# A projection's products and its weight's load moved behind the support's, in the first row group of a two-layer graph-attention kernel

## The chip, the cores and the metric

The kernel runs on one core of one Trainium2 chip. The metric is the device time of one execution in microseconds (us). A profiled execution gives a trace beside it, from which the views below are taken. The engines are PE (TensorE; PEld is its weight load), DVE (VectorE), ACT (ScalarE), POOL (GpSimd) and SP (SyncE, which here only issues DMAs). L841 means line 841 of the kernel before.

## The reference, cut to what matters

Two graph-attention layers over 4096 nodes with 512 features, each followed by a residual and a layer norm. Only the first layer's projections are touched by the change:

```python
support = (x @ weight).reshape(N, H, D)          # 4096x512 by 512x512, 4 heads of 128
f1, f2  = support . weight_u,  support . weight_v  # two numbers per node and head
attn    = masked softmax of leaky_relu(f1 + f2), masked by adj
out     = attn @ support + bias + x @ proj_w + proj_b
x1      = layernorm(x + out)
...                                              # then layer 2: masked multi-head attention, layernorm
```

So `x` is multiplied by two 512x512 weights. The product with `weight` (called "s", the support) feeds everything that follows in layer 1. The product with `proj_w` (called "b", the base) is only added at the end of layer 1; the kernel adds an identity to `proj_w` first, so that the base is the residual too.

## The kernel before, in words

**Stages.** Stage 1 computes supports, bases and attention factors, in eight groups of 512 rows (`g` from 0 to 7, loop at L902). Stage 2 is layer 1's attention: 16 passes (4 windows of 1024 rows, 4 heads) whose products are L1062. Then come layer 2's projections (L1171, L1178) and its attention (L1113, L1375). Beside stage 1 the adjacency is read, cast to 16 bits by a DMA that POOL issues (`narrow`, L589) and transposed by a DMA that SP issues (`turn_in0`, L595), for stage 2.

**A group of stage 1.** Each 512x512x512 product is made from seven half-size products instead of eight (Strassen's scheme). They have the numbers 1 to 7; `("s", 5)` is number 5 of the support. One of them is four matmuls in the source, which the trace shows as eight instructions of 128x256. The products take, besides plain blocks of `x` and of the weights, sums of blocks:

- `combine_x(g, 0..3)` makes four sums of blocks of the group's transposed `x`: 0 and 1 on DVE (L792, L794), 2 and 3 on POOL (L796, L799). Products 5, 6, 7 and 3 need the sums 0, 1, 2 and 3.
- `combine_w` makes four sums of weight blocks once, in the order 5, 6, 7, 4 (L758): for the support on DVE, for the base on POOL. Products 5, 6, 7 and 4 need one each. `add_identity` (L885) must have been over `proj_w` before the base's sums are made; it is 16 additions of 32x32 on POOL.
- Product 2 is added to product 1 in the same PSUM tile, 3 to 5, and 4 to 7. Between the two, the first must have been copied out or read: 1 and 5 by ACT (L858), 7 by DVE (L864). Then ACT (2, L860) and DVE (6, L862; 3 and 4, L869) take the results into the support tile `s4` or the base tile `base`; the last block also needs an addition on POOL (L866). There are six PSUM tiles for the eight that a group uses.
- `dots` (L812) computes the two attention numbers of each node and head from `s4`, on DVE, in four calls of eight operations; each call needs one block of `s4`, the third one the block that POOL's L866 finishes. `turn_x` (L735) transposes the next group's `x` on DVE, in four steps; product 1 of that group needs the first two, its `combine_x` all four.
- POOL adds the bias `bb` to `base` (L873), and SP stores it (L875).

The order on every engine is written out by hand: the lists `begin` (group 0), `usual` and `end` give the order of the 14 products of a group, with counter `k`; each product brings its own copies and additions, and the other steps hang on `k`. An engine takes its instructions in that order. `Later` holds functions until a number of its steps has passed; `step()` is called at four values of `k`.

**Loads at the start.** SP issues the first group's `x` in two halves of four DMAs, and then the `x` of groups 1 and 2. ACT issues sixteen DMAs for the two weights (first half of `weight`, first half of `proj_w`, second halves in the same order; a half is four DMAs of 128 KB) and three more for `uv` and `bias`, all ahead of its first computing instruction. DMAs that SP and ACT issue share eight completion counters, so that a later DMA waits on its engine until an earlier one has landed.

Of the kernel before, what the change touches and what calls it, by code (L numbers as in the profile page):

```python
# [8 lines left out]
F32 = mybir.dt.float32  # L9
# [9 lines left out]
P = 128  # L19
# [410 lines left out]
def tile_gat_then_masked_attention(  # L430
# [16 lines left out]
    nc = tc.nc  # L447
    N, D = x.shape
# [4 lines left out]
    NG = N // G  # L453
# [35 lines left out]
    base_d = [dram.tile([P, GT, D], F32, name=f"base_d{g}") for g in range(NG)]  # L489
# [59 lines left out]
    later = Later()  # L549
# [20 lines left out]
    with tc.tile_pool(name="l0", bufs=NG) as l0, \  # L570
# [71 lines left out]
        with tc.tile_pool(name="l0s", bufs=2) as sp:  # L642
            w_sb, pw_sb = (sp.tile([P, KC, D], F32, name=n, bufs=1) for n in ("w_sb", "pw_sb"))
# [3 lines left out]
            def load_x(g, b0=0, b1=G // SQ):  # L647

                if g not in ys:
                    ys[g] = sp.tile([P, G // SQ, P], F32, name="y_sb", bufs=3)  # L650
                for a in range(NQ):
                    nc.sync.dma_start(
                        ys[g][a * SQ:(a + 1) * SQ, b0:b1, :],
                        x[g * G + b0 * SQ:g * G + b1 * SQ, a * P:(a + 1) * P].rearrange(
                            "(b r) f -> r b f", r=SQ))

            def load_w0(dst, src, c):

                for a in range(NQ):
                    f = a * P + 2 * c * SQ  # L660
                    nc.scalar.dma_start(
                        dst[a * SQ:(a + 1) * SQ, 2 * c:2 * c + 2, :],
                        src[f:f + 2 * SQ, :].rearrange("(k r) d -> r k d", r=SQ))

            bb = sp.tile([P, D], F32, name="bb", bufs=1)
            for n in range(2):
                load_x(0, n * HG // SQ, (n + 1) * HG // SQ)
            for c in range(2):
                for dst, src in ((w_sb, weight), (pw_sb, proj_w)):
                    load_w0(dst, src, c)  # L670
            for k, src in enumerate((weight_u, weight_v)):
                nc.scalar.dma_start(uv[:, k, :], on_all_partitions(src, D))
            nc.scalar.dma_start(bb, on_all_partitions(bias, D))
# [127 lines left out]
            def x_of(g, i):  # L801
                if i in (1, 2, 4):
                    return x_block(g, *{1: (0, 0), 2: (0, 1), 4: (1, 1)}[i])
                return x_s[g][{5: 0, 6: 1, 7: 2, 3: 3}[i]]
# [11 lines left out]
            tiles, base = {}, {}  # L816
# [13 lines left out]
            def product(g, s4, kind, i):  # L830

                if i in (1, 5, 6, 7):
                    tiles[kind, i] = op.tile([P, G], F32, name="o_ps")
                out = tiles[kind, {2: 1, 3: 5, 4: 7}.get(i, i)]
                more = i in (2, 3, 4)
                xb, wb = x_of(g, i), w_of(kind, i)
                for t in range(2):
                    for c in range(2):  # L840
                        nc.tensor.matmul(out[:, t * HD:(t + 1) * HD], xb[:, c, t * P:(t + 1) * P],  # L841
                                         wb[:, c, :], start=not more and t == 0 and c == 0,
                                         stop=c == 1, skip_group_check=True)
                if i == 1:
                    if kind == "b":
                        for n in range(2):
                            base[n] = sp.tile([P, 2, D], F32, name="base", bufs=2)
                    elif g == NG - 1:
                        places = room("y_sb").rearrange("p s c r -> p s (c r)")
                        sb.update({("s", 1): places[:, 0], ("s", 5): places[:, 1],  # L850
                                   ("b", 1): places[:, 2], ("b", 5): places[:, 3]})
                    else:
                        sb.update({("s", 1): room("z"), ("s", 5): room("z"),
                                   ("b", 1): room("az"), ("b", 5): room("az")})
                u2, p5 = sb[kind, 1], sb[kind, 5]
                last = block_of(kind, s4, 1, 1)
                if i in (1, 5):
                    nc.scalar.activation(sb[kind, i], out, AF.Copy)  # L858
                elif i == 2:
                    nc.scalar.activation(block_of(kind, s4, 0, 0), as_block(out, kind), AF.Copy)  # L860
                elif i == 6:
                    nc.vector.tensor_tensor(u2, out, u2, op=ALU.add)  # L862
                elif i == 7:
                    nc.vector.tensor_tensor(last, as_block(out, kind), as_block(u2, kind),  # L864
                                            op=ALU.add)
                    nc.gpsimd.tensor_tensor(last, last, as_block(p5, kind), op=ALU.add)  # L866
                else:
                    n, m = (0, 1) if i == 3 else (1, 0)
                    nc.vector.tensor_tensor(block_of(kind, s4, n, m), as_block(out, kind),  # L869
                                            as_block(u2, kind), op=ALU.add)  # L870
                if kind == "b" and i in (3, 4):
                    n = (3, 4).index(i)
                    nc.gpsimd.tensor_tensor(base[n], base[n],  # L873
                                            bb[:, None, :].to_broadcast([P, 2, D]), op=ALU.add)
                    nc.sync.dma_start(base_d[g][:, 2 * n:2 * n + 2, :], base[n])  # L875

            for n in range(2):
                for c in range(KC):
# [1 line left out]
            def add_identity(m):  # L880
                for c in range(KC):
                    for a in range(2 * m, 2 * m + 2):
                        q, f = slice(a * SQ, (a + 1) * SQ), a * P + c * SQ
                        d = pw_sb[q, c, f:f + SQ]
                        nc.gpsimd.tensor_tensor(d, d, ident[q, q], op=ALU.add)  # L885

            add_identity(0)
            combine_x(0, 0)
            combine_w(nc.vector, "s", (5,))
            for i in (1, 2, 3):  # L890
                combine_x(0, i)
            combine_w(nc.vector, "s", (6, 7, 4))
            add_identity(1)
            combine_w(nc.gpsimd, "b", (5, 6, 7, 4))
            nc.gpsimd.dma_start(bb, on_all_partitions(proj_b, D), accum_op=ALU.add)
            uv_ps = [xp.tile([P, H0, D0], F32, name="x_ps") for _ in range(2)]
            usual = [(kind, i) for i in (1, 5, 2, 6, 7, 3, 4) for kind in ("s", "b")]
            begin = [("s", 1), ("b", 1), ("s", 2), ("b", 2), ("s", 5), ("s", 6), ("s", 7),
                     ("b", 5), ("s", 3), ("b", 6), ("s", 4), ("b", 7), ("b", 3), ("b", 4)]
            end = [("s", 1), ("b", 1), ("s", 5), ("s", 2), ("s", 6), ("s", 7), ("b", 5),  # L900
                   ("s", 3), ("b", 2), ("s", 4), ("b", 6), ("b", 7), ("b", 3), ("b", 4)]
            for g in range(NG):  # L902
                fs[g] = l0.tile([P, 2, GT, H0], F32, name="f")
                s4 = sp.tile([P, H0, GT, W0], F32, name="s4")
                plan = end if g == NG - 1 else usual if g else begin
                todo = {}
                for i, wait, n, m in ((2, 1, 0, 0), (3, 0, 0, 1), (7, 3, 1, 1), (4, 0, 1, 0)):
                    todo.setdefault(plan.index(("s", i)) + wait, []).append((n, m))
                for k, (kind, i) in enumerate(plan):
                    if k in (0, 3, 7, 10):  # L910
                        t = (0, 3, 7, 10).index(k)
                        if t == 1 and g + 2 < NG:
                            load_x(g + 2)
                        for fn in beside.get(g * GT + t, []):
                            fn()
                    product(g, s4, kind, i)
                    if g == 0 and k == 2:
                        for n in range(2):
                            nc.scalar.activation(uv_ps[n], uv[:, n, :].rearrange(
                                "p (h d) -> p h d", h=H0), AF.Copy)  # L920
                    for nm in todo.get(k, ()):
                        dots(g, s4, *nm)
                    first = 0 if g else 10
                    if g + 1 < NG and first <= k < first + KC:
                        turn_x(g + 1, k - first)
                    if g + 1 < NG and (6 <= k < 10 if g else k == 13):
                        for n in (k - 6,) if g else range(4):
                            combine_x(g + 1, n)
                    if k in (2, 6, 9, 13):
                        later.step()  # L930
                xTs.pop(g)
                x_s.pop(g)
                if g + 1 < NG:
                    later.at(1, lambda g=g, s4=s4: factors(g, s4))
                else:
                    factors(g, s4)
# [18 lines left out]
        with wait_by_tile("l0v", 2) as vp:  # L955
# [95 lines left out]
            for n, (w, h, j) in enumerate(steps):  # L1051
# [8 lines left out]
                s = sup[w * H0 + h, j // GT][:, j % GT, :]  # L1060
# [11 lines left out]
    with wait_by_tile("l1", 1) as l1, wait_by_tile("l1a", 2) as lp, \  # L1072
# [46 lines left out]
        with wait_by_tile("l1s", 2) as sp:  # L1119
# [125 lines left out]
            for pair in range(NG // 2):  # L1245
# [4 lines left out]
                if pair == 0:  # L1250
                    combine_features(nc.vector, 0, 3)
                    combine_features(nc.vector, 0, 4)
                    for i in (5, 1, 6, 7):
                        todo = beside.setdefault(order[order.index(i) - 3], [])
# [36 lines left out]
        with wait_by_tile("l1w", 2) as wp, wait_by_tile("l1o", 1, space=PSUM) as op:  # L1291
            NB = 3
            later = Later()
# [274 lines left out]
```

## Time and profile before

| | |
|---|---|
| three runs | 3372.57 us median (3371.79 to 3374.13) |
| the profiled execution | 3370.89 us, of which the span that its trace covers is 3369.1 us |
| PE busy | 3324.9 us, 99% of the span |
| DVE, POOL, ACT busy | 70%, 66%, 59% |
| granted TensorE clock, mean | 0.996 of full speed |
| group 0 of stage 1 | first matmul at 8.76 us, group 1's first at 48.28 us |
| stage 2's first products | 226.99 us; without further stalls from 263.45 us |

Every time below is counted from the span's start. In the timeline a row is: start, duration, engine, line, operation, tile written and tiles read, count; in brackets the idle time of the engine ahead of it, and what ended that idle time. A "q" after an engine marks instructions of its queue, such as the issue of a DMA. In the list of waits a row is: who waited, for whom, then total us, number of times, longest. In the table by windows a row is: window, its length, then for PE, PEld, DVE, ACT and POOL the busy us with the number of instructions, then the granted PE clock, the share of the 16 DMA engines that was busy and the GB/s moved.

### The profile page before, as it was taken

What the parts mean: (1) busy time and instruction counts of PE and PEld (TensorE: products, weight loads), DVE (VectorE), ACT (ScalarE), POOL (GpSimd) and SP (SyncE); (2) the same over time, 40 slices, a digit from 0 to 9 for tenths busy, and PEclk for the clock granted to TensorE, in tenths of its full rate; (3) what the DMA queues carried; (4) which work ended last, traced back from release to release, by engine and by line L of the source; (5) the groups of instructions that cost most, each with busy time, mean ns of one, the idle gap of its engine ahead of it and who ended that gap; (6) DMA issues with size and microseconds to landing.
All of it is one profiled execution on the core that took longest, in us unless ns stands there. A gap on an engine that the chain in (4) does not pass through costs nothing.

```text
span 3369.1 us, 66595 instructions
## 1 busy us (share of the span) xinstructions
PE 3324.9 (99%) x27050; PEld 1950.0 (58%) x27050; DVE 2358.5 (70%) x2892; ACT 1987.4 (59%) x2463; POOL 2226.1 (66%) x1590
## 2 busy tenths in 40 slices
PE   7999999999999999999999999999999999999998
PEld 6889999999999855543333333333333333333332
DVE  5678899898899711157766667676676767667676
ACT  1247877878776421156665656666566656656554
POOL 5540031040030275579999999999999999999996
PEclk9999999999999999999999999999999999999999
DMA  7969869769451443388989898889989889898884
GB/s 162 228 153 177 202 188 218 150 155 215 138 140 64 92 171 112 115 224 195 210 192 222 226 211 195 204 200 237 216 188 213 194 203 253 189 210 190 209 196 111
DMA packets 399054, 620.41 MB, mean 184 GB/s; under 512 B 166672, under 2 KB 247568, under 8 KB 397712
## 3 DMA queue, kind: packets, MB, share of 16 engines
q0 software_dynamic: 97520, 258.77, 42.3%
q1 hardware_dynamic: 298976, 353.35, 34.5%
q10 hardware_dynamic: 2240, 3.93, 0.5%
q8 instruction: 215, 3.52, 0.4%
q14 instruction: 103, 0.84, 0.1%
HBM read 315.87 MB, written 117.64 MB: 129 GB/s over the span
## 4 chain that ended last, share of the span: by engine, by line
PE 89%; DMA 1%; DVE 1%; POOL 1%; issue 0%; ACT 0%; POOLq 0%; DVEq 0%; ACTq 0%
PE o_ps L1062 26%; PE o_ps L1375 25%; PE s_ps L1113 25%; PE s_ps L1178 5%; PE s_ps L1439 3%; PE s_ps L1171 3%; DMA p<-p 1%; PE s_ps L1394 1%; PE x_ps L1043 0%; POOL q_sum L1350 0%; DVE p L637 0%; DMA stage<-adj_d 0%; DVE p L1507 0%; PE x_ps L1171 0%; POOL p L1360 0%
## 5 line engine op out<-in xcount | busy, mean ns | idle before, releaser
L1350 POOL TENSOR_TENSOR q_sum<-q_sum,p 128x1024 f32<-128x1024 f32 x538 | 1376.2, 2558 | 62.6 <-DMA p<-p 38.9
L1330 DVE TENSOR_TENSOR p<-s_ps,adjT 128x1024 f32<-128x1024 f32 x896 | 1043.5, 1215 | 467.2 <-ACT s_ps L1327 443.6
L1327 ACT ACTIVATE s_ps<-s_ps 128x1024 f32<-128x1024 f32 x1021 | 967.2, 1006 | 594.9 <-PE s_ps L1113 594.2
L1375 PE MATMUL o_ps<-p,v_sb 64*64 64x512 f32 x8192 | 943.6, 590 | 0.0
L1113 PE MATMUL s_ps<-q_sb,k_sb 64*64 64x512 f32 x8192 | 943.1, 589 | 0.5 <-DVE p L1330 0.4
L1062 PE MATMUL o_ps<-sup_t,p 128*128 128x129 f32 x8192 | 920.9, 275 | 2.4 <-DVE p L637 2.2
L1062 PEld LDWEIGHTS o_ps<-sup_t,p 128*128 128x128 f32 x8192 | 918.5, 192 | 3.1 <-DVE p L637 3.0
L637 DVE SCALAR_TENSOR_TENSOR p<-fr_t,dj,az 128x1024 f32<-128x1024 f32 x512 | 655.7, 1291 | 78.8 <-PE o_ps L1062 50.6
L1113 PEld LDWEIGHTS s_ps<-q_sb,k_sb 64*64 64x64 f32 x8192 | 312.5, 133 | 567.0 <-issue 453.1
L1375 PEld LDWEIGHTS o_ps<-p,v_sb 64*64 64x64 f32 x8192 | 310.3, 133 | 570.6 <-issue 560.6
L628 ACT ACTIVATE z<-fr_t,f 128x1024 fp8e4<-128x1024 f32 x512 | 558.1, 1144 | 125.9 <-DVE az L632 125.4
L1360 POOL DMA_DIRECT2D p<-p x412 | 438.5, 1304 | 10.2 <-PE o_ps L1375 8.5
L1026 POOL DMA_DIRECT2D agg<-base_d x32 | 28.7, 1206 | 516.0 <-ACT agg L1012 515.8
L1330 DVE TENSOR_TENSOR p<-s_ps,md 128x1024 f32<-128x1024 f32 x128 | 150.7, 1216 | 67.3 <-ACT s_ps L1327 62.7
L632 DVE TENSOR_TENSOR az<-adjT,z 128x512 int32<-128x512 int32 x256 | 175.6, 686 | 11.2 <-ACT z L628 10.4
L588 POOL COPY seen<-token 128x1 f32<-128x1 f32 x24 | 13.4, 557 | 246.2 <-DVE token L586 246.2
L1185 ACT ACTIVATE sb<-s_ps 128x1024 f32<-128x1024 f32 x35 | 35.8, 1024 | 191.8 <-PE s_ps L1178 129.1
L601 ACT ACTIVATE adjT<-stage 128x1024 fp8e4<-128x1024 bf16 x128 | 130.4, 1049 | 6.3 <-DMA stage<-adj_d 6.3
L1200 POOL TENSOR_TENSOR sb<-sb,sb 128x1024 f32<-128x1024 f32 x36 | 84.9, 2374 | 71.8 <-ACT sb L1185 71.8
L1224 DVE COPY k_sb<-s_ps 128x1024 f32<-128x1024 f32 x12 | 14.7, 1225 | 140.7 <-PE s_ps L1178 90.6
L1439 PE MATMUL s_ps<-wo_sb,on 128*128 128x512 f32 x240 | 110.8, 604 | 0.0
L1409 ACT ACTIVATE r<-r_h 32x256 f32<-32x256 f32 x248 | 102.3, 412 | 2.9
(176 smaller groups left out, 2135.4 us busy)
## 6 DMA issues: line engine op xcount, KB each, us to landing
p<-p POOLq DMA_DIRECT2D x412, 512.0 KB, 9.1
k_sb<-k_d SPq DMA_DIRECT2D x128, 512.0 KB
v_sb<-v_d SPq DMA_DIRECT2D x128, 512.0 KB
adj_d<-in_adj_dram POOLq DMA_DIRECT2D x32, 1024.0 KB, 11.3
sup_t<-sup_d SPq DMA_DIRECT2D x120, 258.0 KB
fr_t<-fr_d SPq DMA_DIRECT2D x16, 1024.0 KB
adjT_d<-adjT SPq DMA_DIRECT2D x32, 512.0 KB
adjT<-adjT_d SPq DMA_DIRECT2D x32, 512.0 KB
```

What stands on the lines that cost most here:

```text
L628: nc.scalar.activation(z[:, k, :], fr[:, 0, :], AF.Sign, bias=fs[j // GT][:, 0, (j + k) % GT, h:h + 1], saturate=False)
L632: nc.vector.tensor_tensor(az.bitcast(I32), adjT[w, j // CJ][:, j % CJ:j % CJ + 2, :].bitcast(I32), z.bitcast(I32), op=ALU.bitwise_and)
L637: nc.vector.scalar_tensor_tensor(p, fr[:, 1, :], dj[j // GT][:, j % GT, h:h + 1], az_t[w, h, j // 2][:, j % 2, :], op0=ALU.max, op1=ALU.mult)
L1062: nc.tensor.matmul(o[t // BK][:, t % BK, :], p[:, t * P:(t + 1) * P], s, start=(j == 0 and t % BK == 0), stop=(j == NT - 1), skip_group_ch ...
L1113: nc.tensor.matmul(s[c:c + MS, e, :], k[r, a + c:a + c + MS], qt[g, m][r, :], start=True, stop=True)
L1178: nc.tensor.matmul(half, a[:, c, n * P:(n + 1) * P], x[:, c, :], start=not more and c == 0, stop=c == 1, skip_group_check=True)
L1327: nc.scalar.activation(s, s, AF.Exp)
L1330: nc.vector.tensor_tensor(p, s, keep[:, None, :].to_broadcast([P, HP, G]), op=ALU.mult)
L1350: nc.gpsimd.tensor_tensor(q, q, p, op=ALU.add)
L1360: later.at(2, lambda: nc.gpsimd.dma_start(a, b, accum_op=ALU.add))
L1375: nc.tensor.matmul(o[c, n, :], v[r, j % CH, c], p[r, e, :], start=(j == 0), stop=(j == NT - 1))
L1439: nc.tensor.matmul(s, on_t[g][:, m, t * P:(t + 1) * P], wo_sb[:, m, :], start=(m == 0), stop=(m == NP1 - 1))
```

## The change

- `begin` lists all seven support products first, then the seven of the base, each in the order 1, 2, 5, 6, 7, 3, 4. Before, the two kinds alternated. The copy of `uv` to PSUM moves from `k` = 2 to `k` = 6, and the four calls of `dots` of group 0 to `k` = 7, 8, 9 and 10.
- `proj_w` is loaded from SP's queue, after `x` of group 0 and ahead of `x` of groups 1 and 2. ACT's queue keeps `weight`, `uv` and `bias`.
- All 16 additions of the identity come after POOL's `combine_x(0, 2)` and `(0, 3)`; eight of them stood ahead of those before.
- The store of a `base` half is handed to `Later` with one step, and the last of the four steps of a group is called at `k` = 12 instead of 13 (with one more after group 7). `base` has three buffers instead of two.

```diff
-            for c in range(2):
-                for dst, src in ((w_sb, weight), (pw_sb, proj_w)):
-                    load_w0(dst, src, c)
+            for queue, dst, src in ((nc.scalar, w_sb, weight), (nc.sync, pw_sb, proj_w)):
+                for c in range(2):
+                    load_w0(queue, dst, src, c)
...
-                            base[n] = sp.tile([P, 2, D], F32, name="base", bufs=2)
+                            base[n] = sp.tile([P, 2, D], F32, name="base", bufs=3)
...
-                    nc.sync.dma_start(base_d[g][:, 2 * n:2 * n + 2, :], base[n])
+                    later.at(1, lambda t=base[n]: nc.sync.dma_start(
+                        base_d[g][:, 2 * n:2 * n + 2, :], t))
...
-            add_identity(0)
             combine_x(0, 0)
             combine_w(nc.vector, "s", (5,))
             for i in (1, 2, 3):
                 combine_x(0, i)
             combine_w(nc.vector, "s", (6, 7, 4))
-            add_identity(1)
+            for m in range(2):
+                add_identity(m)
             combine_w(nc.gpsimd, "b", (5, 6, 7, 4))
...
-            begin = [("s", 1), ("b", 1), ("s", 2), ("b", 2), ("s", 5), ("s", 6), ("s", 7),
-                     ("b", 5), ("s", 3), ("b", 6), ("s", 4), ("b", 7), ("b", 3), ("b", 4)]
+            begin = [(kind, i) for kind in ("s", "b") for i in (1, 2, 5, 6, 7, 3, 4)]
...
-                for i, wait, n, m in ((2, 1, 0, 0), (3, 0, 0, 1), (7, 3, 1, 1), (4, 0, 1, 0)):
-                    todo.setdefault(plan.index(("s", i)) + wait, []).append((n, m))
+                for k, (i, wait, n, m) in enumerate(
+                        ((2, 1, 0, 0), (3, 0, 0, 1), (7, 3, 1, 1), (4, 0, 1, 0))):
+                    todo.setdefault(plan.index(("s", i)) + wait if g else 7 + k, []).append((n, m))
...
-                    if g == 0 and k == 2:
+                    if g == 0 and k == 6:
                         for n in range(2):
                             nc.scalar.activation(uv_ps[n], uv[:, n, :].rearrange(
                                 "p (h d) -> p h d", h=H0), AF.Copy)
...
-                    if k in (2, 6, 9, 13):
+                    if k in (2, 6, 9, 12):
                         later.step()
                 xTs.pop(g)
                 x_s.pop(g)
+                if g + 1 == NG:
+                    later.step()
```

More of the change, by code (lines that the diff above doesn't have):

```diff
@@ L655, in load_x, with load_w0 @@
                             "(b r) f -> r b f", r=SQ))
-            def load_w0(dst, src, c):
+            def load_w0(queue, dst, src, c):
                 for a in range(NQ):
                     f = a * P + 2 * c * SQ
-                    nc.scalar.dma_start(
+                    queue.dma_start(
                         dst[a * SQ:(a + 1) * SQ, 2 * c:2 * c + 2, :],
```

## The prediction

> **What bounds the kernel now.** I read the page's busy shares first, then the table by windows cut at the stages, then the waits and the timeline of the first 60 us, and the chain of waits up to 270 us. The page says that PE is the bound; the table says where it isn't:
>
> ```profile
> PE 3324.9 (99%) x27050; PEld 1950.0 (58%) x27050; DVE 2358.5 (70%) x2892; ACT 1987.4 (59%) x2463; POOL 2226.1 (66%) x1590
> ```
> ```profile
> 0.00:48.28 48.28, 30.13 (x112) 24.64 (x113) 19.93 (x88) 5.77 (x9) 16.91 (x35) 0.89 0.84 153
> 48.28:215.90 167.62, 167.62 (x777) 147.25 (x775) 110.19 (x517) 51.16 (x94) 100.28 (x89) 1.00 0.91 202
> 215.90:263.45 47.55, 37.68 (x298) 36.36 (x297) 38.86 (x82) 27.37 (x31) 14.83 (x10) 0.89 0.66 158
> 263.45:1157.00 893.55, 893.43 (x8000) 893.23 (x8000) 805.90 (x907) 680.25 (x761) 122.41 (x169) 1.00 0.69 154
> ```
>
> Group 0 ends at 48.28. Up to there PE is busy 30.13 of 48.28 us; from there to 215.9 it never stops, so groups 1 to 7 follow group 0's end one for one. What the change reorders lies in that first window, and what holds PE there is in the timeline:
>
> ```profile
> 8.76 3.78 PE L841 MATMUL o_ps<-w_sb,xT 128*128 128x256 f32 x8 [8.76 <-DVE xT L735]
> 12.79 2.79 PE L841 MATMUL o_ps<-pw_sb,xT 128*128 128x256 f32 x8 [0.26 <-DMA pw_sb<-in_L_gnn_proj_w_dram]
> 21.10 1.28 ACT L858 ACT_TABLE_LOAD   x1 [21.10 <-DMA pw_sb<-in_L_gnn_proj_w_dram]
> 22.40 0.60 ACT L858 ACTIVATE z<-o_ps 128x512 f32<-128x512 f32 x1
> 23.05 3.78 PE L841 MATMUL o_ps<-w_sb,xT 128*128 128x256 f32 x8 [7.46 <-ACT z L858]
> ...
> 46.48 1.97 PE L841 MATMUL o_ps<-more_w,xT 128*128 128x256 f32 x8 [1.68 <-DVE base L864]
> ```
>
> PE does s1 and b1, then stands 7.46 us, because s2 goes into s1's PSUM tile and ACT has not copied s1 out; ACT can't before 21.10, because it is still issuing loads. From 23.05 PE runs nearly without a stop to 48.28 (1.68 us for DVE at b4), the first 5 us of it at half the clock.
>
> **What the Trainium skill says.** (1) "TensorE: Matmul & The Clock Gate", Part 1: the PE clock is at half until some 3.4 us of sustained work, and falls back after an idle window. The trace agrees: eight matmuls took 3.78 us at 8.76 and again at 23.05, after the stall, and 1.89 us in the steady stretch. (2) The same page, queue depths: ACT, DVE and POOL take instructions strictly in order. The trace agrees: ACT's first copy waits 21.10 us behind DMA issues that it doesn't need. (3) "DMA: Bandwidth & Descriptors", "Issuing engines are not separate DMA queues": SP's and ACT's DMAs share 16 engines, so moving a load to another queue saves issue time, not bandwidth. Agrees: the DMA share is over 1.0 in each microsecond from 3 to 30, at some 200 GB/s.
>
> **The change, part by part.**
>
> *Load of `proj_w` off ACT's queue.* Eight issues leave ACT. `weight`'s second half takes the places 5 to 8, whose issues went at 3.73 to 7.83 and whose last landing released b1 at 12.79; `uv`, `uv`, `bias` take the places 9 to 11, issued at 8.65, 10.02 and 11.28. ACT is free at about 11.6, its table load (1.28) ends at 12.9, the copy of s1 at 13.5. So s2 starts at about 13.6 instead of 23.05. Cost on SP: eight more issues at 0.32 us, and the queue moved past is `x` of groups 1 and 2. Both are hidden if the data is there in time: before, all 6 MB had landed by 31; the bytes are the same, so `x` of group 1 lands at some 27 and of group 2 at some 31 to 33, against needs at about 34 and 38.
>
> *Support products first.* DVE makes the sums as before from 13.48 (arrival of `x`'s second half), one per 0.6 us in the order x0, w5, x1, w6, w7, w4: ready at 15.6, 16.2, 16.8, 17.4, 18.0, 18.6. POOL, with no identity ahead, has x2 at 16.2 and x3 at 18.1. At full clock (1.73 us a product, as from 32.55 to 39.46) s5 runs from 16.3, s6 from 18.0, then s7, s3, s4 to 24.9. If the clock stays low for s2 and part of s5, to about 26.4. Both ends are kept.
>
> *Base products.* POOL's chain: 16 identity additions at 0.3 us from 18.1 to 22.9. `proj_w` now shares the engines with 0.75 MB of `uv` and `bias`; 3.9 MB at 200 GB/s from 2 us puts its last piece at about 21.5, the additions that need it come at 21.7. Then four sums (27.39 to 32.48 before, 5.1 us) to 28.0, the `bb` DMA's issue (1.08) to 29.1, and L866 of the support (1.08) to 30.2. PE: b1 from 24.9 to 26.6; b2 must wait for ACT's copy of b1 out of the same tile, a new stall of about 0.75 us, to 29.1 in all; b5, b6, b7, b3 to 36.0 (their sums are ready from 24.2 to 28.0); b4 needs DVE's read of b7; to 37.7.
>
> *Dots later on DVE.* Eight pairs at 0.21 us, 1.67 us a call. Calls 1 and 2 go from 25.8 to 29.2; call 3 waits for POOL's L866 until 30.3 and is a new wait with DVE's queue behind it: b6's addition (0.6), call 4 (1.7), a transpose (0.6), b7's addition (0.6, done 35.5), a transpose (done 36.1). So b4 may start at 35.5 (PE arrives at 36.0), and group 1's product 1, which needs two transposes, at 36.1 (PE arrives at 37.7). DVE is just off the path, by 0.5 us.
>
> *Stores a step later, third buffer.* On SP the order of stores is what it was, but for one: the second base store of group 3 falls behind the load of `fr_t`. Nobody on the path waits for either; no wait of L860 or L864 on a store shows before 230 us. Cost and gain nothing; if the cover failed, a base store's landing is some us in the middle of a PE-bound stretch that has 24 us per group.
>
> *Sum.* Group 1's first product at 37.7 (clock high early) to 39.2 (low), against 48.28: 9.1 to 10.6 us. I take 39.0, since POOL and DVE slow each other a little (L873 took 2.81 and 2.36 us): a gain of 9.3 us. Groups 1 to 7 (167.6 us of unbroken PE) carry it. At the transition the chain is
>
> ```profile
> 237.80 3.08 DVE p L637 x2
> 241.84 11.37 DMA stage<-adj_d
> ```
>
> and this transpose stood on SP behind stores of POOL's products of group 7 (L695 to 238.6), so it moves with the group. From 263.45 PE is the bound again. The profiled execution goes from 3370.89 to 3361.6; the median of the runs was 1.68 above it, so 3363.3.
>
> **Rivals.**
>
> *A. As above,* 3361 to 3365.
>
> *B. POOL's chain is later.* If `proj_w` lands at 26 to 28 instead of 21.5, because it shares with `uv` and stands behind `x`, the identity ends 4 to 5 us later, L866 and call 3 with it, DVE is the bound, and group 1 starts at about 42 to 44: gain 4 to 6, 3367.5. For it: POOL waited 18.7 us for `proj_w` before. Against: then it was last of 16 loads on ACT's queue, in step with `x` of groups 1 and 2, and its last quarter's additions needed no wait after 24.94; now it is ahead of that `x`.
>
> *C. The shift is not carried through.* DMA is at 1.0 to 1.1 of its share between 90 and 180 us; if the casts and transposes of the adjacency already ran at their own pace, stage 2 would start when they are done, whatever group 0 does: 3370 to 3373. Against: no engine waits for a DMA between 60 and 230 us, the casts are issued by POOL as the groups go (8.1 to 14.8 us to landing, with 24 us a group), so they move too.
>
> *D. Slower.* One mechanism: call 3 of `dots` holds DVE for POOL, which is held by `proj_w`. Group 1 starts about 14.3 us after the last identity addition (5.1 + 1.1 + 1.1 for POOL, 7.0 for DVE and b4). It is a loss once that addition is later than 34 us, a measurable one from 40.7, each us of delay one us. It takes SP's queue holding `proj_w` until everything else has landed (31 us) and 10 us more; at 43 the time would be 3382.
>
> *E. It does something else than it says.* The order of instructions on each engine shows the products, dots and loads moved as described, and the stores hardly moved; that last part is the one that does nothing.
>
> **Chances.** A 0.74, B 0.14, C 0.08, D 0.04. A measurement of this kernel can tell about 0.2%, 6.7 us, from no change: the line is at 3365.8 (and 3379.3). A is faster; B is mostly within (0.04 of it faster); C within (0.01 faster); D slower. So faster 0.79, same 0.17, slower 0.04. The range: from 10.6 us of gain and 1.5 us of spread, 3360.5, up into B, 3368.5; C and D are left out.
>
> **What would show it.** ACT's table load at about 12 instead of 21.10. s2 at about 13.6, with a wait on ACT under 1.5 us. The last identity addition at about 23, L866 of the support at about 30. DVE's third call behind POOL for about 1 us. b2 with 0.7 us of wait on ACT. Group 1's first `w_sb` product at 38 to 39, PE without idle from there on to about 206, and the stage 2 start at 254. I am wrong if POOL's first addition on `proj_w`'s last quarter waits beyond 24 us (B, or D beyond 34), if turn_x of group 1 waits for `x`, or if the transposes at the transition start no earlier than 241.

## The result and the profile after

The changed kernel takes 3365.62 us (median of 8 runs, 3362.72 to 3366.93), the kernel before 3372.77 us beside it (8 runs, 3371.53 to 3374.34): a ratio of 0.9977, with a 95% interval of 0.9967 to 0.9988, so 7.15 us less. The profiled execution of the changed kernel took 3366.7 us, its span is 3364.9 us; it is one of the longer of its runs, which matters below.

The line of busy time from the page is almost what it was. PE does the same work in a span 4.2 us shorter:

```profile
PE 3323.4 (99%) x27050; PEld 1947.6 (58%) x27050; DVE 2360.0 (70%) x2892; ACT 1987.3 (59%) x2463; POOL 2226.0 (66%) x1590
```

The table by windows of the changed kernel, cut at the same events as before (group 1's first product, the end of the unbroken stretch of PE, the start of stage 2's free stretch, layer 2's first projection). After the window come its length, then busy time and instructions of PE, PEld, DVE, ACT and POOL, then PE's clock, the DMA share and GB/s:

```profile
0.00:39.81 39.81, 28.88 (x112) 23.72 (x113) 21.40 (x88) 5.88 (x9) 18.10 (x35) 1.00 1.03 183
39.81:207.40 167.59, 167.59 (x777) 147.25 (x775) 110.17 (x517) 51.15 (x94) 100.26 (x89) 1.00 0.91 203
207.40:255.01 47.61, 36.97 (x298) 35.62 (x297) 38.80 (x82) 27.37 (x31) 14.83 (x10) 0.93 0.67 158
255.01:1150.05 895.04, 893.42 (x8001) 893.23 (x8001) 807.47 (x910) 681.18 (x766) 123.66 (x171) 1.00 0.70 154
```

The prediction's row for the last window of the kernel before ended at 1157.00, 0.2 us ahead of layer 2's first projection. Cut at that projection, it reads:

```profile
263.45:1157.20 893.75, 893.43 (x8000) 893.24 (x8001) 806.06 (x909) 680.45 (x762) 122.61 (x169) 1.00 0.69 154
```

Window 1 is 8.47 us shorter than before (48.28), windows 2 and 3 are as long as before, and window 4 is 1.29 us longer with the same PE work in it (893.42 against 893.43). (PE's clock of 1.00 in the first row doesn't speak of the first products: so early the trace holds no record of the clock, and the durations below show them at half speed.) So the whole gain is made in group 0, it is carried through groups 1 to 7 and the transition, and a part of it is given back at the end of layer 1.

The timeline of the changed kernel's first 40 us, PE and ACT (start, duration, engine and line, operation; in brackets the idle time just before and what ended it):

```profile
8.71 3.78 PE L841 MATMUL o_ps<-w_sb,xT 128*128 128x256 f32 x8 [8.71 <-DVE xT L735]
11.68 1.28 ACT L858 ACT_TABLE_LOAD   x1 [11.68 <-DMA w_sb<-in_L_gnn_weight_dram]
12.97 0.60 ACT L858 ACTIVATE z<-o_ps 128x512 f32<-128x512 f32 x1
13.62 3.78 PE L841 MATMUL o_ps<-w_sb,xT 128*128 128x256 f32 x8 [1.13 <-ACT z L858]
17.20 3.95 PE L841 MATMUL o_ps<-fr_t,p 128*128 128x256 f32 x16
28.79 1.97 PE L841 MATMUL o_ps<-pw_sb,xT 128*128 128x256 f32 x8 [0.73 <-POOL pw_sb L758]
38.01 1.97 PE L841 MATMUL o_ps<-more_w,xT 128*128 128x256 f32 x8 [0.35 <-DVE base L864]
39.81 1.89 PE L841 MATMUL o_ps<-w_sb,xT 128*128 128x256 f32 x8
```

ACT is free of its loads at 11.68 instead of 21.10, PE's stall before s2 is 1.13 us instead of 7.46, and b4's 1.68 has become 0.35. The stall of 0.73 us at b2, which the prediction expected on ACT, is there. The profile puts it down to POOL, whose sum into `pw_sb` ended at 28.62, but b2 doesn't read the block that this sum writes. By the program b2 waits for ACT's copy of b1 out of the same tile (28.09 to 28.69); in the last but one experiment below, where POOL's sums end at other times, the profile does name ACT for this stall (0.69 us).

The lead over the kernel before, read at events of the two traces:

| event | before, us | after, us | lead |
|---|---|---|---|
| group 1's first product | 48.28 | 39.81 | 8.47 |
| start of stage 2's free stretch | 263.45 | 255.01 | 8.44 |
| layer 2's first projection (first matmul of L1178, after: L1181) | 1157.20 | 1150.05 | 7.15 |
| PE's matmul 13080, in layer 2's attention | 1769.20 | 1763.95 | 5.25 |
| PE's last matmul | 3355.60 | 3351.56 | 4.04 |

Two losses stand after group 0: 1.3 us up to layer 2's first projection, and 3.1 us in layer 2's attention. In the second place PE waits 3.2 us in all, at four matmuls, for DVE's L1333, which itself waits for accumulating DMAs (DMAs that add to what the tile holds). Before the change it was 0.4 us. The longest of the four waits is at matmul 13080 (counted from 0):

```profile
1762.67 2.35 DVE L1333 TENSOR_TENSOR p<-s_ps,adjT 128x1024 f32<-128x1024 f32 x2 [3.00 <-DMA p<-p]
1763.95 1.09 PE L1116 MATMUL s_ps<-q_sb,k_sb 64*64 64x512 f32 x8 [1.73 <-DVE p L1333]
```

The same places in the profiles of the experiments, which are described below (one profile of each kernel; line numbers differ by a few). The last column is the time from layer 2's first projection to PE's last two matmuls:

| kernel | later stores, third `base` buffer | wait at matmul 13080, us | all waits for L1333, us | layer 2, us |
|---|---|---|---|---|
| before | no | 0 | 0.4 | 2198.37 |
| queue alone | no | 0 | 0 | 2197.90 |
| stores as before | no | 0 | 0.4 | 2198.52 |
| the changed kernel | yes | 1.73 | 3.2 | 2201.48 |
| order alone | yes | 1.61 | 3.7 | 2202.35 |
| other banks | yes | 1.35 | 1.5 | 2199.55 |
| b6 ahead of b5 | yes | 1.36 | 2.2 | 2201.18 |
| `proj_w` behind `x` | yes | 1.56 | 1.8 | 2199.87 |
| identity as before | yes | 1.63 | 1.6 | 2199.51 |
| further version | yes | 1.82 | 3.7 | 2202.62 |

So the wait at this one matmul goes with one part of the change, the later stores with their third buffer: it is in all seven profiles that have it and in none of the three that don't, and layer 2 is 1.0 to 4.7 us longer on PE in the seven. Of the three, "stores as before" alone has the new order of products too, so this one profile is what tells the stores from the order. How that part comes to a wait 1.5 ms later isn't shown. The other waits for L1333 follow no edit that is known. The whole times don't show the wait: the medians of the changed kernel and of the program that runs it again (3365.62 and 3364.38) are no longer than that without this part (3365.61, third experiment).

Here is the first of the two losses, the 1.3 us at the entry of layer 2, in the timeline, before and after:

```profile
1156.26 1.40 ACT L1012 ACTIVATE agg<-o_ps,rinv 128x128 f32<-128x128 f32 x5 [13.11 <-DVE rinv L1008]
1157.20 3.70 PE L1178 MATMUL s_ps<-xT,wk_low 128*128 128x512 f32 x8 [0.32 <-ACT agg L1012]
```
```profile
1147.82 1.40 ACT L1015 ACTIVATE agg<-o_ps,rinv 128x128 f32<-128x128 f32 x5 [13.11 <-DVE rinv L1011]
1149.03 0.39 ACTq L1078 DMA_DIRECT2D wo_sb<-in_L_gnn_Wo_dram  x1
1149.09 0.91 ACT L1015 ACTIVATE agg<-o_ps,rinv 128x128 f32<-128x128 f32 x3
1150.05 3.70 PE L1181 MATMUL s_ps<-xT,wk_low 128*128 128x512 f32 x8 [1.61 <-ACT agg L1015]
```

ACT copies the last eight results of layer 1 out of three PSUM tiles. Before, the first projection of layer 2 starts while the first five are under way; after, it starts 0.05 us after the last of the eight, which come behind a load that ACT issues in between. The stall went from 0.32 to 1.61 us.

### The profile page after: what moved, and what is told of

Its sections match the earlier page's. It is cut to its first block, busy times and chain, and to the rows that moved or that the text cites. A ratio compares the mean times of both kernels' runs of the same rounds, so it can differ in the third digit from the quotient of the medians.

```text
span 3364.9 us, 66591 instructions
## 1 busy us (share of the span) xinstructions
PE 3323.4 (99%) x27050; PEld 1947.6 (58%) x27050; DVE 2360.0 (70%) x2892; ACT 1987.3 (59%) x2463; POOL 2226.0 (66%) x1590
## 4 chain that ended last, share of the span: by engine, by line
PE 81%; issue 6%; DMA 3%; POOL 2%; DVE 1%; ACT 0%; POOLq 0%; DVEq 0%
PE o_ps L1378 24%; PE s_ps L1116 24%; PE o_ps L1065 20%; PE s_ps L1181 5%; PE s_ps L1442 3%; PE s_ps L1174 3%; DMA p<-p 2%; POOL q_sum L1353 1%; PE s_ps L1397 1%; DVE p L637 0%; POOL p L1363 0%; DMA xT<-x1T_d 0%; DMA stage<-adj_d 0%; PE x_ps L1046 0%; DVE p L1333 0%
## 5 line engine op out<-in xcount | busy, mean ns | idle before, releaser
L1333 DVE TENSOR_TENSOR p<-s_ps,adjT 128x1024 f32<-128x1024 f32 x896 | 1043.4, 1215 | 469.8 <-ACT s_ps L1330 442.0
L1333 DVE TENSOR_TENSOR p<-s_ps,md 128x1024 f32<-128x1024 f32 x128 | 150.8, 1217 | 67.7 <-ACT s_ps L1330 63.0
```

Of the source, the lines that this page charges most:

```text
L1333: nc.vector.tensor_tensor(p, s, keep[:, None, :].to_broadcast([P, HP, G]), op=ALU.mult)
```

## The experiments

In each experiment "group 1 at" and "layer 2's first projection at" give the start of that matmul on PE in the profile of its kernel: group 1's first product is at 39.81 in the changed kernel and at 48.28 before, layer 2's first projection at 1150.05 and 1157.20. The edits are shown against the changed kernel, but for the queue alone, which is shown against the kernel before. A range behind a time is the fastest and the slowest run; a ratio is to the kernel before, with its 95% interval. The runs of the kernel before that stood beside them had a median of 3372.57 us for the first four experiments and of 3371.97 us for the last four.

**The queue alone.** The load of `proj_w` goes to SP's queue; products, identity, dots and stores are as before.

```diff
-            def load_w0(dst, src, c):
+            def load_w0(queue, dst, src, c):
...
-                    nc.scalar.dma_start(
+                    queue.dma_start(
...
-            for c in range(2):
-                for dst, src in ((w_sb, weight), (pw_sb, proj_w)):
-                    load_w0(dst, src, c)
+            for queue, dst, src in ((nc.scalar, w_sb, weight), (nc.sync, pw_sb, proj_w)):
+                for c in range(2):
+                    load_w0(queue, dst, src, c)
```

> Only the load of proj_w moves to SP's queue; order, identity and stores are those of before. My theory (the two main parts need each other): ACT is free at 12, but b1 now stands ahead of s2 on PE and waits for proj_w's first half, which lands at about 17 to 18, so s2 starts at about 21, not at 13.6; group 1 starts at about 46 instead of 48.28: gain about 2 us, 3371. Rival (freeing ACT is the whole gain, the order only follows): group 1 at about 40, gain 7 to 8, 3365.

Measured: group 1 at 45.05; 3369.06 us (3367.33 to 3373.32, 13 runs), ratio 0.9993 (0.9985 to 1.0002). PE in its timeline:

```profile
17.98 3.75 PE L841 MATMUL o_ps<-pw_sb,xT 128*128 128x256 f32 x8 [5.61 <-DMA pw_sb<-in_L_gnn_proj_w_dram]
21.52 2.77 PE L841 MATMUL o_ps<-w_sb,xT 128*128 128x256 f32 x8
43.24 1.97 PE L841 MATMUL o_ps<-more_w,xT 128*128 128x256 f32 x8 [1.69 <-DVE base L864]
```

The stall is not gone, it has another cause: b1 stands ahead of s2 and now waits for `proj_w`, which comes later on SP's queue. That ACT is free at 11.7 is of no use to a PE that stands before b1.

**The order alone.** All of the change but the queue.

```diff
-            for queue, dst, src in ((nc.scalar, w_sb, weight), (nc.sync, pw_sb, proj_w)):
-                for c in range(2):
-                    load_w0(queue, dst, src, c)
+            for c in range(2):
+                for dst, src in ((w_sb, weight), (pw_sb, proj_w)):
+                    load_w0(nc.scalar, dst, src, c)
```

> The changed kernel with proj_w on ACT's queue again, in the old order of the loads; support-first order, identity and stores as changed. My theory: ACT is free only at 21.1, s2 starts at 23.05 as before, and PE then has 13 products ahead where before had 12; no 1.68 us stall at b4, a new one of 0.7 at b2: group 1 at about 49, 0.7 us later than before, and 1.3 us more is lost at the start of layer 2 as in the changed kernel: 3374 to 3375. Rival (the order is the whole gain): group 1 at about 40 to 42, 3366.

Measured: group 1 at 49.19; 3375.34 us (3371.15 to 3376.98, 13 runs), ratio 1.0006 (0.9998 to 1.0014). The wait for ACT is now the longest in group 0, as b1 no longer fills a part of it:

```profile
23.07 3.78 PE L841 MATMUL o_ps<-w_sb,xT 128*128 128x256 f32 x8 [10.48 <-ACT z L858]
```

At group 1 the queue alone is worth 3.2 us and the order alone costs 0.9; together they are worth 8.5. Neither part is the cause by itself: the queue frees ACT, and the order keeps PE from standing before products that need the load which now comes later. In the whole time neither part alone can be told from the kernel before (both intervals hold 1); together they take 7.15 us off it.

**The stores as before.** The changed kernel with the base stores, the buffers of `base` and the steps as they were.

```diff
-                            base[n] = sp.tile([P, 2, D], F32, name="base", bufs=3)
+                            base[n] = sp.tile([P, 2, D], F32, name="base", bufs=2)
...
-                    later.at(1, lambda t=base[n]: nc.sync.dma_start(
-                        base_d[g][:, 2 * n:2 * n + 2, :], t))
+                    nc.sync.dma_start(base_d[g][:, 2 * n:2 * n + 2, :], base[n])
...
-                    if k in (2, 6, 9, 12):
+                    if k in (2, 6, 9, 13):
...
-                if g + 1 == NG:
-                    later.step()
```

> The changed kernel without the later stores, the third base buffer and the moved step. My theory: nothing moves; group 1 at 39.8, stage 2's stretch without stalls from 255.0, and the 1.3 us that the changed kernel gives back at its first layer-2 projection (PE waits 1.6 us for ACT's copies there, 0.3 before) is still given back: 3365.6, equal to the changed kernel within 1. Rival (the later stores or the third buffer shift what layer 2 waits for): the wait there is 0.3 us again and the time 1.3 us less, or, if the third buffer saved a wait, the time is longer.

Measured: group 1 at 39.34; 3365.61 us (3364.48 to 3370.45, 13 runs), ratio 0.9981 (0.9973 to 0.999). In the median this part of the change does nothing that can be measured. It isn't the cause of the loss at the entry of layer 2 either; the waits of PE there show the same 1.6 us:

```profile
PE s_ps L1178 <- ACT agg L1012: 1.6, 1, 1.6
```

What it does change, in the profile, is the wait at matmul 13080, which is gone. This profile's lead over the kernel before is 7.3 us at layer 2's first projection and still 7.1 at PE's last matmul, where the changed kernel's fell from 7.15 to 4.04. About half of these 3.1 us is lost again in this profile, as its end behind PE's last matmul took 14.9 us instead of 13.3. Why nothing of it is left in the medians stays open.

**Other banks for the last results: an edit that missed.** It was to place the three PSUM tiles of layer 1's last pass differently.

```diff
+                    if (w, h) == passes[-1]:
+                        o_t[w, h] = o_t[w, h][2:] + o_t[w, h][:2]
```

> The changed kernel with one edit at the last pass of layer 1: its three result tiles change places, so that the first of them, not the last, lies in the PSUM banks that layer 2's first tile takes. My theory (the new order of group 0 shifts which bank each later tile gets, and that alone gives back 1.3 us): PE's wait at the first layer-2 projection falls from 1.6 to about 0.3 us, the lead over before stays at 8.4 us there, and the time is about 1.3 us under the changed kernel, 3364.3. Rival (ACT's copies are late for another reason): the wait stays at 1.6 us and the time at 3365.6.

Measured: group 1 at 39.10, the wait still 1.6 us, layer 2's first projection at 1149.05; 3364.38 us (3362.76 to 3367.07, 12 runs), ratio 0.9979 (0.997 to 0.9988). In the built program the tiles lie where they lay: banks go by the order of first use, and turning the list round changes only names. So it tells nothing about the banks; it is the changed kernel once more, and says how far such medians scatter: 3365.62 and 3364.38 for the same program, 1.2 us. It also says how far a profile of group 0 does: group 1 came 0.7 us earlier here, with s2 at 1.99 us instead of 3.78 (the last section comes back to it).

**b6 ahead of b5 in group 0.** In the changed kernel POOL has the weight sums of both (done at 27.38) before the first of the two products starts (30.59), so the exchange costs group 0 nothing, but it exchanges the PSUM tiles of two products. In the built programs, layer 2's first tile takes banks 0 and 1. Layer 1's last three tiles lie in banks 1, 5, 2 before the change, in 5, 4, 0 after it, and in 5, 4, 2 with this edit (in 5, 4, 3 in the further version below).

```diff
-            begin = [(kind, i) for kind in ("s", "b") for i in (1, 2, 5, 6, 7, 3, 4)]
+            begin = [("s", i) for i in (1, 2, 5, 6, 7, 3, 4)] + \
+                [("b", i) for i in (1, 2, 6, 5, 7, 3, 4)]
```

> The changed kernel with base products 5 and 6 of group 0 in the other order. That costs group 0 nothing that I can see (group 1 at 39.5 to 40), but it changes which PSUM bank each later tile gets: in the built program layer 2's first projection then waits for no copy of the last pass, where in the changed kernel it waits for all eight, and in the kernel before for three. My theory (the 1.3 us given back at the start of layer 2 is that wait): PE's wait there falls from 1.6 us to 0.3 or less, the lead over before at the first layer-2 projection is 8.4 to 8.8 us instead of 7.15, and the time is 1.3 to 1.6 us under the changed kernel, 3364.2. Rival (that wait only stands where another would): another wait, for DVE or a DMA, takes its place and the lead stays at 7.2.

Measured: layer 2's first projection at 1146.22, with no wait; 3363.54 us (3360.02 to 3369.65, 9 runs), ratio 0.9976 (0.9966 to 0.9986). In the timeline PE now starts while ACT copies, 1.7 us ahead of the end of the last copy (1147.94):

```profile
1145.77 1.40 ACT L1016 ACTIVATE agg<-o_ps,rinv 128x128 f32<-128x128 f32 x5 [13.11 <-DVE rinv L1012]
1146.22 3.60 PE L1182 MATMUL s_ps<-xT,wk_low 128*128 128x512 f32 x8
1147.03 0.91 ACT L1016 ACTIVATE agg<-o_ps,rinv 128x128 f32<-128x128 f32 x3
```

The lead over the kernel before goes from 10.50 us at stage 2's free stretch (252.95 against 263.45) to 10.98 here, where the changed kernel lost 1.3. So the cause is shown in the trace: order in group 0 shifts the rotation of the banks, and with it which copies the first projection waits for. In the whole time it is not established: this median is 2.1 us under the changed kernel's, but only 0.8 under the run before it, which has the changed kernel's banks. And the 1.4 us that this profile is ahead at group 1 (38.37 against 39.81) aren't the edit's: `x` was ready 0.75 us earlier (12.70 against 13.45), and s2 ran at full clock. A later wait, for POOL's L1146, grew from 0.7 to 1.1 us; the lead behind it is 10.73, so a quarter of a us comes back.

**`proj_w` behind `x` of group 1.** The place on SP's queue, at which the prediction's rivals B and D turn.

```diff
-            for queue, dst, src in ((nc.scalar, w_sb, weight), (nc.sync, pw_sb, proj_w)):
-                for c in range(2):
-                    load_w0(queue, dst, src, c)
+            for c in range(2):
+                load_w0(nc.scalar, w_sb, weight, c)
...
             load_x(1)
+            for c in range(2):
+                load_w0(nc.sync, pw_sb, proj_w, c)
```

> The changed kernel with proj_w loaded on SP's queue behind x of group 1 instead of ahead of it, so 1 MB later. My theory (proj_w is on the path through POOL: identity, four sums, L866, then the third dots call on DVE; group 1 starts 15.1 us after the last identity addition, as in the changed kernel, 24.7 and 39.8): proj_w lands some 5 us later, the last identity addition is at 29 to 30, group 1 at 44 to 45, and the time is about 5 us more than the changed kernel's, 3370.5. Rival (PE's own products set group 0's end, POOL has room): group 1 at 40 to 41, 3366.

Measured: last identity addition done at 28.11, group 1 at 44.34; 3370.51 us (3368.3 to 3373.74, 13 runs), ratio 0.9994 (0.9985 to 1.0002). First a row from the waits of its first 50 us, then two of the timeline:

```profile
DVE prod L813 <- POOL s L867: 5.7, 1, 5.7
```
```profile
34.01 1.39 POOL L867 TENSOR_TENSOR s<-s,z 128x512 f32<-128x512 f32 x1
40.80 3.75 PE L842 MATMUL o_ps<-more_w,xT 128*128 128x256 f32 x8 [3.80 <-DVE base L865]
```

POOL's addition ends 7.3 us after the last identity addition, as rival D had it. DVE stands 5.7 us for it, PE 3.8 us for DVE. From the identity to group 1 it is 16.2 us against D's 14.3, and 1.8 of that is b4 at half clock after the stall (3.75 us against 1.97; the granted clock from 40.80 to 44.34 was 0.50). The mechanism of B and D is real: here the last identity addition came 3.4 us later than in the changed kernel (24.69) and group 1 came 4.5 us later. The change as written puts the load early enough: the same stretch takes 15.1 us in it, and PE is busy for nearly all of that.

**The identity as before.** `add_identity(0)` ahead of POOL's first sums again.

```diff
+            add_identity(0)
             combine_x(0, 0)
...
-            for m in range(2):
-                add_identity(m)
+            add_identity(1)
```

> The changed kernel with the first eight identity additions ahead of POOL's sums of x again, as in the kernel before. My theory: they wait for proj_w's pieces until 19.9, x sums 2 and 3 come at 21.3 and 22.5 instead of 15.6 and 19.1, still ahead of products 7 and 3 at 22.7 and 24.4, and the last addition at 25.0 instead of 24.7: group 1 at 39.5 to 40.3, time equal within 1 us, 3365.6. Rival (moving the identity back was needed): s7 waits, group 1 at 42 or later, 3368.

Measured: group 1 at 40.25; 3366.16 us (3364.16 to 3369.16, 21 runs), ratio 0.9983 (0.9976 to 0.9989). This part is worth 0.4 us in the trace and nothing that the medians can tell.

**A version that goes further.** Three small edits on the changed kernel: b6 and b2 exchanged, so that b2 doesn't follow b1 in its tile; the last weight sum and the `bb` load behind POOL's addition for which DVE waits; the dots two at a time, behind products 7 and 8 instead of 7 to 10.

```diff
-            combine_w(nc.gpsimd, "b", (5, 6, 7, 4))
-            nc.gpsimd.dma_start(bb, on_all_partitions(proj_b, D), accum_op=ALU.add)
+            combine_w(nc.gpsimd, "b", (5, 6, 7))
...
+            begin = [("s", i) for i in (1, 2, 5, 6, 7, 3, 4)] + \
+                [("b", i) for i in (1, 6, 5, 2, 7, 3, 4)]
...
-                    todo.setdefault(plan.index(("s", i)) + wait if g else 7 + k, []).append((n, m))
+                    todo.setdefault(plan.index(("s", i)) + wait if g else 7 + k // 2, []).append((n, m))
...
+                    if g == 0 and k == 4:
+                        combine_w(nc.gpsimd, "b", (4,))
+                        nc.gpsimd.dma_start(bb, on_all_partitions(proj_b, D), accum_op=ALU.add)
```

> The changed kernel, the base products of group 0 in the order 1, 6, 5, 2, 7, 3, 4 (no stall between 1 and 2, and the PSUM banks as in the run with 6 ahead of 5), the fourth base sum and the load of proj_b on POOL behind its addition for the support (L866), and the four dots calls at k = 7, 7, 8, 8. My theory: L866 ends at 29.7 instead of 32, DVE's third call doesn't wait, b2 doesn't wait for ACT's copy of b1, PE is the bound in group 0's second half: group 1 at 38.3 instead of 39.8, and with the wait at layer 2's start gone the time is 2.9 us under the changed kernel, 3362.7. Rival (DVE bounds it anyway): group 1 stays at 39.5, 3364.

Measured: group 1 at 37.94; 3362.57 us (3359.62 to 3363.67, 7 runs), ratio 0.9967 (0.9955 to 0.9978): 9.4 us under the kernel before, the lowest median of the study. It is 3.05 us under the changed kernel, which ran beside another set of runs of the kernel before; the trace shows 1.9 us of it at group 1 (0.3 of them at s5, by the clock), and at the entry of layer 2, where the first projection waits for no copy, it loses none of the 1.3 us that the changed kernel loses there. In its timeline

```profile
16.86 3.72 PE L841 MATMUL o_ps<-fr_t,p 128*128 128x256 f32 x16 [1.21 <-DVE fr_t L758]
27.47 1.99 PE L841 MATMUL o_ps<-more_w,p 128*128 128x256 f32 x8
28.60 1.10 POOL L866 TENSOR_TENSOR s<-s,z 128x512 f32<-128x512 f32 x1
36.21 1.89 PE L841 MATMUL o_ps<-more_w,xT 128*128 128x256 f32 x8
```

the profile marks no stall between 16.86 and group 1: what follows b1 has a tile of its own, POOL's addition starts at 28.60 instead of 30.60, and b4 waits for nobody. In this execution PE waits 1.21 us for DVE's first weight sum instead of running s2 at half clock.

## Why the prediction was right, and where its numbers were off

The mechanism is the one of case A, though 3365.62 us lies 0.6 above the 3361 to 3365 that stand there for it, and only 0.2 under the 3365.8 up to which the prediction called the kernel faster. The terms, one by one:

- *ACT off its loads*: table load at 11.68 (11.6 predicted), copy at 12.97 (12.9), s2 at 13.62 (13.6), stall 1.13 us (under 1.5). Right. That it takes both parts is what the first two experiments add: the prediction's sum has the gain for both together and doesn't say that the queue alone would leave PE standing at b1.
- *Support sums on DVE and POOL*: s5 at 17.20 (16.3 at high clock). Its sums did not hold it: the one that it needs from DVE was done at 16.72. What held it is s2, whose eight matmuls took 3.78 us, the low clock that the prediction kept as its other end; b1 at 26.16 lies inside its 24.9 to 26.4. But the sums were late too. The prediction let DVE and POOL add side by side at their single rates, and the trace shows them waiting for each other. DVE and POOL in the timeline, the lone additions before, then the changed kernel:

```profile
14.93 0.69 DVE L792 TENSOR_TENSOR p<-xT 128x512 f32<-128x512 f32 x1
```
```profile
14.31 1.27 POOL L796 TENSOR_TENSOR p<-xT 128x512 f32<-128x512 f32 x1 [12.87 <-DVE xT L735]
14.91 1.21 DVE L792 TENSOR_TENSOR p<-xT 128x512 f32<-128x512 f32 x1
17.41 1.65 POOL L799 TENSOR_TENSOR p<-xT,p 128x512 f32<-128x512 f32 x1 [1.83 <-DVE p L794]
17.85 1.75 DVE L758 TENSOR_TENSOR w_sb<-w_sb 128x512 f32<-128x512 f32 x1
19.02 5.67 POOL L886 TENSOR_TENSOR pw_sb<-pw_sb,ident 32x32 f32<-32x32 f32 x16
```

  The Trainium skill has the reason, which the prediction did not use: "SBUF — State Buffer", "SBUF: two separate sides", says that a DVE operation with two SBUF inputs and a GpSimd operation that reads SBUF take a shared port pair in turn, each for its whole length, and the other blocks. The trace agrees: DVE's L792 starts at 14.91 beside POOL's L796, which ends at 15.58, and is itself done at 16.12, some 0.54 us after POOL; DVE's L758 at 17.85 is done 0.54 us after POOL's L799 ends (19.06). So POOL's sum x2 (L796) cost DVE 0.5 us at the head of its weight sums and x3 (L799) 1.1 us further on, while x3 itself took 1.65 us instead of 1.27. In this execution it was POOL's chain that paid for it, not PE.
- *POOL's chain*: identity from 19.02 to 24.69 (18.1 to 22.9 predicted), so 1.8 us late: 0.9 from the same lock ahead of it, 0.9 within it (16 additions in 5.67 us, 0.3 us each predicted), which isn't traced to a cause. `proj_w` was no wait at all: it had landed, as predicted. Nor did group 1's `x` hold anything. L866 ended at 31.99 (30.2), and DVE waited 1.6 us for it (about 1).
- *b2's new stall*: 0.73 us (0.75). Right.
- *Group 1*: 39.81 against 39.0, with a computed 37.7 to 39.2. From b1 to group 1 it took 13.65 us instead of 12.8. The term that was mis-sized is DVE's margin at b4: it was to clear DVE by 0.5 us and missed it by 0.35, as L866 and the third call of `dots` came late. The rest lies in products beside the two stalls, 1.80 to 1.90 us apart instead of 1.73. Those 13.65 us repeat (13.65 and 13.66 in the third and fourth experiments, the same path), but b1's start moves with the clock: group 1 was at 39.81, 39.34 and 39.10 in the three. So 39.0 was near, and 0.8 is what one execution missed it by.
- *Stores, third buffer*: nothing. Right in the medians, by the third experiment. In the profiles it isn't nothing: the waits of 1.4 to 1.8 us at matmul 13080 go with this part. The prediction looked for such a wait only ahead of 230 us.
- *The carry*, "Groups 1 to 7 (167.6 us of unbroken PE) carry it" and "From 263.45 PE is the bound again": the first held to 0.03 us (8.47 to 8.44), the start of stage 2 is at 255.01 (254). The second failed by 1.3 us, by a term that the sum didn't have: the tile rotation that ends layer 1 in banks which layer 2 needs first. In the profile it failed again, by the waits in layer 2's attention.

Together: the profiled execution was forecast at 3361.6 and took 3366.7. The 5.1 us between are, to 0.1, the sum of the 0.8 in group 0, the 1.3 at the entry of layer 2 and the 3.1 in its attention. In the median 9.27 us of gain were predicted and 7.15 measured, and there the first two, 2.1 us, would do alone. That they fit so well is partly luck: they come from one profile, the 0.8 was 0.3 and 0.1 in the two other profiles of the same path, the wait at matmul 13080 isn't in this sum though it was in every profile with the later stores, and the interval of the medians (4 to 11 us of gain) is wider than any of them. The range held, by its mechanism; that the median came within 2.3 us of the 3363.3 says little of the small terms.

Rival B's 42 to 44 for group 1 and C's unmoved transition are refuted by 39.81 and by the transpose in the chain, which starts at 233.28 (241.84 before):

```profile
233.28 11.48 DMA stage<-adj_d
```

D did not come about; the sixth experiment shows its mechanism, though not so far that it made the kernel slower. What stays open: whether the 1.3 us of the banks can be seen in the whole time; how the later stores and the third buffer come to a wait in layer 2, and whether it costs anything in the median; and what sets the other waits in layer 2's attention.

## What to carry to other kernels

When a load leaves an engine's queue, look at which product stands next on the consumer: freeing ACT was worth 3.2 us until the products that need the delayed load were moved behind those that don't, and 8.5 after. An order that is changed in one place moves every later use of a rotating pool, so look at the first instruction of the next stage and ask which copies hold its tile. When two-input additions of DVE and POOL are planned side by side, don't count on their single rates: here two of DVE's took 1.21 and 1.75 us instead of 0.69. And a part of a change that moves no median can still move a wait far away from it. To see that, follow one and the same instruction through the profiles of kernels with that part and without it, before calling a wait chance.

## What the runs showed of the hardware that was not expected

- The clock after a short gap is decided by the execution, not by the kernel. The same eight matmuls of s2, after gaps of 0.7 to 1.4 us, took 3.78 us in the changed kernel and 1.99 us in four of the experiments (other banks, b6 ahead of b5, `proj_w` behind `x`, the further version). The first of these is the changed kernel's own program:

```profile
13.61 1.99 PE L841 MATMUL o_ps<-w_sb,xT 128*128 128x256 f32 x8 [1.35 <-ACT z L858]
```

  The Trainium skill's "TensorE: Matmul & The Clock Gate", Part 1, says that the window that decides is free-running and doesn't start with the kernel. That fits, but no run here shows the window itself. Between those two executions it made 0.7 us at group 1 (39.81 against 39.10), less than the 1.8 us of s2 because s5 then waited 1.10 us for DVE's sum.
- A stall on PE is paid twice: 3.80 us of waiting at b4 in the sixth experiment brought 1.8 us more of half clock in b4 (granted clock 0.50), and 1.1 us more in the product behind it (3.02 us against 1.89).
